# A four-layer graph network on one core: node steps one to a group and tied behind the group's messages, carried sums on TensorE, ranks by a predicated copy

## The chip, the cores and the metric

The kernel runs on one core of one Trainium2 chip. The metric is the device time of one execution in microseconds. The profiled execution of the kernel before took 5402.67 us and its span, from the first to the last instruction that the profiler saw, is 5400.9 us. Engine names are those of the profile: PE is TensorE (PEld its weight loads), DVE is VectorE, ACT is ScalarE, POOL is GpSimd, SP is SyncE, which here only issues transfers.

## The reference

The node features `x` are 6250 x 160 (64 scalars and 32 three-vectors a node). There are 100000 edges, each with a source `src` and a target `dst`, and the edges come sorted by `dst`. Four layers follow each other, each of the form `x = x + gnn(relu(layernorm(x)))`. Cut to what the change touches, a layer is

```
gs, gv   = lin1(h)[src]                         # gather a row of a table for each edge
weight   = silu(edge_features @ W_fc1) @ W_fc2  # 192 weights for each edge
edge_msg = [w0*gs*ys, w3*dot(gv, yv), w1*gs*yv, w2*gv*ys]        # 384 numbers an edge
agg      = segment_sum(edge_msg, dst, N)
x        = x + lin2(agg) + skip(h)
```

The third layer (index 2) gathers by `dst` and sums by `src` instead, so that its edges have to be put in the order of `src` first: each edge needs its rank in that order.

## The kernel before

The edges stand in 784 tiles of 128, and 14 tiles make a **window**. All edges of a window point to at most 128 nodes that follow each other, and column 0 of a window is the node that the window before may have begun. There are 56 windows. A **group** is 4 tiles, so that a layer has 196 groups and a window is 3.5 groups long.

Layers 0, 1 and 3 run in `edges(li)`. Its main loop takes one group after the other and records, in this order:

- `prepare` (L1363): the loads of a pair of windows (`load`, SP queue), and the gather of the group that is 6 ahead: 4 indirect transfers of 128 rows on POOL (L1280);
- `weights_of` and `edge_weights`: on PE the hidden layer `ph` (L1269; L1263 in layer 3) and the weights `pw` (L1303; L1296 in layer 3), on ACT the activation (L1272) and the copies to `ws` (L1307, L1309);
- `messages`: seven DVE instructions, the one-hot `oh` (L1322), `pr` (L1333), `dot` (L1334) and four parts of `msg` (L1336, L1339, L1340 and, as the last one recorded, L1341);
- the sum over edges: 4 products `pg` (L1397) with the one-hot as weights. After the last tile of a window ACT copies the sums to `acc` (L1400), and a Python generator `nodes` (L1346) for this window joins the list `live`;
- the node work: each generator in `live` is advanced. Every `yield` in it ends a step.

The steps of a window's node work are, in `nodes` and `nodes_out`: the one-hot `turn` (L1349, DVE) and four products `pt_out` (L1062, PE) that turn and shift `acc`; the copy `at` (L1069, ACT) and the addition of the sums that the window before has left for this window's first node (L1073, DVE: column 0 of the `at` before into column 1 of this one); the products `po` (L1080, L1082, PE); and the update of `xt` (L1095, L1096, DVE; in layer 3 a chain from L1115 on with a sine on ACT, L1135). Layers 0 and 1 go on in `nodes_in` with the next layer's input: statistics (L991, L992, DVE), `norm` with small instructions of 0.15 us to 0.27 us (L886, L969 to L979, L888, DVE), `hn` (L999, ACT), in layer 0 `hk` (L1004, DVE), the transposes `pt_in` (L1009, L1010, PE), their copies `ht` (L1013, L1014, ACT), the products `pa` (L1022, PE), the table's rows `tb` (L1031 or L1033, ACT), and in layer 0 the addition of `pa` to `xt` (L1041, DVE), with the writes to memory on the SP queue (L1034, L1047, L1048). All `pt_out`, `po`, `pt_in` and `pa` tiles share two PSUM buffers.

Beside layers 0 and 1 runs `positions` (L1142), the ranks by `src`. For each of 54 buckets it makes a mask `hit` over all 784 tiles (L1166), a running count `cum` (L1168), and takes the count over where the mask is set by a product and a sum (L1171, L1172). After every third group of layers 0 and 1 one step of it is recorded.

The engines do not run in the order of recording. A scheduler (the tile framework) puts the instructions of each engine in an order when the program is built: of what is ready by its own estimate, what was recorded first goes first. On the chip each engine then works through its fixed order, and an instruction that waits holds up all that is queued behind it. Between layers stands a full dependence: a layer's gathers read the table that the node work before has written, to the last window.

Two stages between layer 1 and layer 3, `messages2` and `sums2`, do the third layer; `sums2` uses `nodes_out` without `turn`.

Of the kernel before, what the change touches and what calls it, by code (L numbers as in the profile page):

```python
# [11 lines left out]
F32 = mybir.dt.float32  # L12
# [3 lines left out]
ALU = mybir.AluOpType  # L16
# [673 lines left out]
class Fast:  # L690
# [360 lines left out]
    def nodes_out(self, li, xt, sk, acc, turn, carry, w, wk, pp):  # L1051
# [5 lines left out]
        for k in range(4):  # L1057
            rows, o = (96, 3 * MV) if k == 0 else (MV, (k - 1) * MV)
            if turn is None:
                nc.tensor.transpose(pt[:rows, k, :], acc[:, o : o + rows], self.ident[:n, :n])  # L1060
            else:
                nc.tensor.matmul(pt[:rows, k, :], lhsT=acc[:, o : o + rows], rhs=turn, start=True, stop=True)  # L1062
        yield
# [4 lines left out]
        else:  # L1068
            nc.scalar.copy(at, pt)  # L1069
        if turn is not None:  # L1070

            if carry[0] is not None:
                nc.vector.tensor_add(at[:, :, 1], at[:, :, 1], carry[0][:, :, 0])  # L1073
            carry[0] = at
        yield
# [66 lines left out]
    def positions(self, wk):  # L1142
# [21 lines left out]
        for b in range(BK + 1):  # L1164
            hit = wk.tile([P, TT], BF16, name="hit2", bufs=2)
            nc.vector.tensor_scalar(hit, self.src_b, float(b), None, op0=ALU.is_equal)  # L1166
            cum = wk.tile([P, TT], F32, name="cum", bufs=2)
            nc.vector.tensor_tensor_scan(cum, hit, self.zero.to_broadcast([P, TT]), self.off[:, b : b + 1], op0=ALU.add,  # L1168
                                         op1=ALU.add)
            yield  # L1170
            nc.vector.tensor_mul(cum, cum, hit)  # L1171
            nc.vector.tensor_add(pos, pos, cum)  # L1172
            yield
# [31 lines left out]
    def edges(self, li):  # L1205
# [31 lines left out]
        def load(u):  # L1237

            rt = ld.tile([P, 2 * WT, 8], F32, name="rt")
            nc.sync.dma_start(rt.rearrange("p t c -> p (t c)"), self.a["rec0"][u])  # L1240
            rows = self.a[f"ft{li}"].shape[1]
            ft = ld.tile([rows, self.a[f"ft{li}"].shape[2]], F32, name="ft")
            nc.sync.dma_start(ft, self.a[f"ft{li}"][u])
            for h in range(2):
                k = 2 * u + h
                at = self.at(k)
                xt = nk.tile([P, XW], F32, name="xt", bufs=10)
                nc.sync.dma_start(xt, self.x[li][ds(at, P), :])
                sk = None
                if li == 3:  # L1250
                    sk = nk.tile([P, 160], F32, name="sk_out", bufs=10)
                    nc.sync.dma_start(sk, self.skip[3][ds(at, P), :])
                xts[k] = xt, sk
            data[u] = rt, ft
# [57 lines left out]
        def messages(u, g):  # L1312
# [27 lines left out]
            tt(mvec[:, :, :, 0:64], by3(t1, 64), yv[:, :, :, None].to_broadcast([P, n, 3, 64]), ALU.mult)  # L1340
            tt(mvec[:, :, :, 64:96], e1, by3(ws[:, :, 64:96], 32), ALU.mult)  # L1341
            return oh, msg

        carry = [None]

        def nodes(k, acc):  # L1346
            xt, sk = xts.pop(k)
            turn = nk.tile([P, P], F32, name="turn")
            nc.vector.tensor_scalar(turn, self.iota, self.column[:, k : k + 1], None, op0=ALU.is_equal)  # L1349
# [35 lines left out]
        for i, (u, g) in enumerate(groups):  # L1385
            prepare(i + AHEAD)
            weights_of(i + 2)
            if i + 1 < len(groups):
                edge_weights(*groups[i + 1])
            oh, msg = messages(u, g)  # L1390
            for k in range(width(u, g)):
# [6 lines left out]
                if end:  # L1398
                    acc = wk.tile([P, AW], F32, name="acc")
                    nc.scalar.copy(acc, pg)  # L1400
                    live.append(nodes(t // WT, acc))
            data.pop(u - 1, None)
            live = [n for n in live if not (next(n, True) or next(n, True))]
            if li < 2 and i % 3 == 0:
# [363 lines left out]
```

## Time and profile before

| what | us |
|---|---|
| three runs | 5421.51, 5421.99, 5408.77; median 5421.51 |
| profiled execution, and its span | 5402.67, 5400.9 |
| before the loop of layer 0 | 0 to 160 |
| layer 0 with its node work | 160 to 1320 |
| layer 1 with its node work | 1320 to 2440 |
| `messages2`, `sums2` | 2440 to 3525, 3525 to 4340 |
| layer 3 | 4340 to 5401 |
| busy over the span | PE 4493.4, DVE 4198.7, ACT 2075.5, POOL 3192.6 |

The start of the last message product of a group (L1341) gives the pace: in layer 0 the first is at 181.6 and the 196th at 1304.7, in layer 1 at 1337.6 and 2414.6, in layer 3 at 4364.5 and 5379.5. Divided by the 195 steps between them that is 5.76, 5.52 and 5.21 us a group.

How to read the views: a group of instructions is one row with its line, engine, operation, tiles and shapes, how many there were, their busy time and the mean of one in ns, and then the idle time of that engine just before them with what ended it. A row of the waits says which instruction waited for which, in total, how often, and the longest. A row of the stages gives a stretch with the busy time (and number) of PE, PEld, DVE, ACT and POOL, then the clock granted to PE as a share of its full one, the DMA share and GB/s. The ends of PE's instructions are modelled, so that PE's busy time says more than its work.

### The profile page before, as it was taken

How to read it: one execution, taken by the hardware profiler on the slowest of the kernel's cores; microseconds unless marked ns; L12 is line 12 of the kernel's file. 1: busy time of each engine (PE TensorE's matmuls, PEld its weight loads, DVE VectorE, ACT ScalarE, POOL GpSimd, SP SyncE). 2: the span in 40 equal slices, each digit the busy share in tenths (PEclk: the TensorE clock that was granted, in tenths of full speed). 3: DMA queues.
4: the chain of work that ended last, by engine and by line, in shares of the span. 5: the costliest groups of instructions: out<-in, count | busy, mean ns of one | idle time of the engine just before them, and what ended most of it. 6: DMA issues, size and time to landing. Idle time of an engine off the chain costs nothing.

```text
span 5400.9 us, 77388 instructions
## 1 busy us (share of the span) xinstructions
PE 4493.4 (83%) x22084; PEld 2812.5 (52%) x22084; DVE 4198.7 (78%) x11742; ACT 2075.5 (38%) x6858; POOL 3192.6 (59%) x3143
## 2 busy tenths in 40 slices
PE   6899999998999999985565565589999988888886
PEld 4455555554455555543443344368888844444443
DVE  6688888987888888975777777767777768878787
ACT  5444444443444444543333333312222244444442
POOL 0577777773777767765777777700000057777776
PEclk9988998988888888986777776689999978888887
DMA  3333333322333333326655656477777533333332
GB/s 96 111 94 92 89 87 89 88 75 69 95 94 89 96 85 91 99 75 201 205 199 201 211 194 207 161 276 238 239 235 237 186 81 84 82 85 85 84 80 58
DMA packets 373006, 708.23 MB, mean 131 GB/s; under 512 B 71469, under 2 KB 250890, under 8 KB 372442
## 3 DMA queue, kind: packets, MB, share of 16 engines
q0 software_dynamic: 163072, 349.43, 22.4%
q1 hardware_dynamic: 208914, 353.42, 21.3%
q8 instruction: 180, 2.95, 0.2%
q14 instruction: 256, 2.10, 0.1%
q10 hardware_dynamic: 584, 0.33, 0.0%
HBM read 493.90 MB, written 209.08 MB: 130 GB/s over the span
## 4 chain that ended last, share of the span: by engine, by line
PE 23%; DVE 11%; DMA 11%; POOL 8%; issue 5%; ACT 2%; SPq 0%; DVEq 0%; ACTq 0%; POOLq 0%
PE pg L1620 7%; DMA rec<-row,edge_to 6%; PE pg L1618 5%; DMA ge<-table,rt 5%; POOL rec L1516 5%; POOL ge L1280 3%; PE pg L1397 2%; DVE msg L1340 2%; PE pa L1022 1%; PE po L1082 1%; DVE msg L1336 1%; DVE row L1509 1%; DVE pr L1333 1%; PE ph L1458 1%; PE pw L1296 1%
## 5 line engine op out<-in xcount | busy, mean ns | idle before, releaser
L1280 POOL DMA_INDIRECT ge<-table,rt x2352 | 2374.6, 1010 | 1878.2 <-DMA skip<-sk 830.3
L1397 PE MATMUL pg<-msg,oh 128*64 128x384 f32 x4704 | 1072.5, 577 | 159.6 <-DVE msg L1341 144.1
L1307 ACT ACTIVATE ws<-pw,rt 128x96 f32<-128x96 f32 x2352 | 691.8, 349 | 843.3 <-DVE msg L1341 320.1
L1516 POOL DMA_INDIRECT rec<-row,edge_to x784 | 817.2, 1042 | 302.3 <-issue 182.1
L1303 PE MATMUL pw<-w_w2y,hh 100*128 100x192 f32 x3136 | 676.7, 358 | 16.5 <-ACT ws L1309 14.1
L1397 PEld LDWEIGHTS pg<-msg,oh 128*64 128x64 f32 x4704 | 310.9, 151 | 721.3 <-issue 262.4
L1303 PEld LDWEIGHTS pw<-w_w2y,hh 100*128 100x128 f32 x3136 | 545.1, 205 | 224.6 <-ACT ws L1309 110.2
L1340 DVE TENSOR_TENSOR msg<-msg,bank 128x768 f32<-128x768 f32 x588 | 556.2, 946 | 0.0
L1620 PE MATMUL pg<-msg,oh 128*120 128x288 f32 x1668 | 541.3, 406 | 0.0
L1336 DVE TENSOR_TENSOR msg<-ws,ge 128x512 f32<-128x512 f32 x588 | 402.7, 685 | 71.6 <-DMA ge<-table,rt 71.3
L1484 PE MATMUL pe<-tb,oh 64*128 64x160 f32 x1568 | 280.3, 416 | 200.8 <-ACT row L1493 198.7
L1618 PE MATMUL pg<-rt,oh 128*120 128x192 f32 x1668 | 410.1, 328 | 35.1 <-DVE oh L1608 35.1
L1272 ACT ACTIVATE hh<-ph 100x1024 f32<-100x1024 f32 (+1 forms) x336 | 269.5, 802 | 406.4 <-PE pw L1296 179.7
L1333 DVE TENSOR_TENSOR pr<-ge,bank 128x384 f32<-128x384 f32 x588 | 320.4, 545 | 125.2 <-DMA ge<-table,rt 124.2
L1484 PEld LDWEIGHTS pe<-tb,oh 64*128 64x128 f32 x1568 | 211.4, 259 | 354.9 <-ACT row L1493 344.7
L1269 PE MATMUL ph<-ft,w_w1r 12*100 12x512 f32 (+1 forms) x784 | 328.9, 666 | 78.5 <-ACT hh L1272 60.2
L1309 ACT COPY ws<-pw 128x192 f32<-128x192 f32 x1176 | 390.4, 332 | 0.0
L1458 PE MATMUL ph<-ft,w_w1d 128*128 128x512 f32 x224 | 176.8, 887 | 239.4 <-ACT hh L1460 215.9
L1618 PEld LDWEIGHTS pg<-rt,oh 128*120 128x120 f32 x1668 | 298.1, 184 | 123.2 <-issue 36.3
L1509 DVE TENSOR_TENSOR row<-pw,ev 128x512 f32<-128x512 f32 x196 | 135.4, 691 | 282.8 <-ACT row L1495 270.2
L1334 DVE TENSOR_REDUCE dot<-pr 128x128 f32<-128x384 f32 x588 | 344.4, 586 | 0.1
L1341 DVE TENSOR_TENSOR msg<-ge,ws 128x384 f32<-128x384 f32 x588 | 324.4, 552 | 0.0
(488 smaller groups left out, 7439.9 us busy)
## 6 DMA issues: line engine op xcount, KB each, us to landing
rt<-rec SPq DMA_DIRECT2D x208, 780.0 KB
ge<-table,rt POOLq DMA_INDIRECT x2352
ft<-in_ft_dram SPq DMA_DIRECT2D x56, 512.0 KB
ft<-in_ft_dram SPq DMA_DIRECT2D x28, 896.0 KB
dt<-in_dst_w_dram SPq DMA_DIRECT2D x112, 224.0 KB
xt<-x SPq DMA_DIRECT2D x168, 82.0 KB
rec<-row,edge_to POOLq DMA_INDIRECT x784
rt<-in_rec_dram SPq DMA_DIRECT2D x84, 112.0 KB
```

The costliest lines, as they stand in the source:

```text
L1280: nc.gpsimd.indirect_dma_start(out=ge[:, k, :], out_offset=None, in_=self.table[li], in_offset=bass.IndirectOffsetOnAxis(ap=rt[:, G * g + ...
L1303: nc.tensor.matmul(pw[:, i, :192], lhsT=hh[:, k + i, :], rhs=w2, start=True, stop=True)
L1307: nc.scalar.activation(ws[:, k0 + i, 0:96], pw[:, i, 0:96], AF.Copy, scale=rt[:, G * g + k0 + i, 0:1])
L1309: nc.scalar.copy(ws[:, k0 : k0 + m, 96:192], pw[:, :m, 96:192])
L1333: tt(pr, e1, yv[:, :, :, None].to_broadcast([P, n, 3, 32]), ALU.mult)
L1336: tt(msg[:, :, AW - 64 : AW + 64].rearrange("p g (k u) -> p g k u", k=2), ws.rearrange("p g (k u) -> p g k u", k=2)[:, :, :, 0:64], e0[:, ...
L1340: tt(mvec[:, :, :, 0:64], by3(t1, 64), yv[:, :, :, None].to_broadcast([P, n, 3, 64]), ALU.mult)
L1397: nc.tensor.matmul(pg[half], lhsT=oh[:, k, :], rhs=msg[:, k, :AW], start=t % WT < 2, stop=t % WT >= WT - 2)
L1484: nc.tensor.matmul(pe[:, 2 * h + k // 2, :160], lhsT=oh[rows, (t0 + k) % WT // 2, :], rhs=tb[rows], start=True, stop=True)
L1516: d = nc.gpsimd.indirect_dma_start(out=self.rec2, out_offset=bass.IndirectOffsetOnAxis(ap=self.edge_to[:, t0 + k : t0 + k + 1], axis=0), i ...
L1618: nc.tensor.matmul(pg[:, 0:192], lhsT=oh[:, k, :], rhs=rt[:, k, 0:192], start=first, stop=end, skip_group_check=True)
L1620: nc.tensor.matmul(pg[:, 192:480], lhsT=oh[:, k, :], rhs=msg[:, k, :], start=False, stop=end, skip_group_check=True)
```

## The change

Three things, all in the part of the program that layers 0, 1 and 3 share.

First, the list `live` is advanced once a group, not twice, and inside a context that puts an ordering edge from the group's last message product to every DVE instruction that the steps record: the scheduler cannot put them in front of it. Instructions of other engines get no edge. Since a window's node work now lasts twice as many groups, its tiles get more buffers (`xt` and `sk_out` 14 for 10, `turn` and `acc` 6 for 2).

Second, the carried sums are no longer added by DVE behind the copy `at`. The generator keeps the window's `acc` and `turn`, and in the next window PE adds, for each of the four parts of `pt_out`, a product of the old `acc` with column 0 of the old `turn` into column 1 of the same PSUM tile.

Third, in `positions` the product and the sum become one predicated copy: where `hit` is not zero, `pos` takes `cum`.

```
             rows, o = (96, 3 * MV) if k == 0 else (MV, (k - 1) * MV)
             if turn is None:
                 nc.tensor.transpose(pt[:rows, k, :], acc[:, o : o + rows], self.ident[:n, :n])
-            else:
-                nc.tensor.matmul(pt[:rows, k, :], lhsT=acc[:, o : o + rows], rhs=turn, start=True, stop=True)
+                continue
+            nc.tensor.matmul(pt[:rows, k, :], lhsT=acc[:, o : o + rows], rhs=turn, start=True, stop=carry[0] is None,
+                             skip_group_check=True)
+            if carry[0] is not None:
+                sums, turned = carry[0]
+                nc.tensor.matmul(pt[:rows, k, 1:2], lhsT=sums[:, o : o + rows], rhs=turned[:, 0:1], start=False,
+                                 stop=True, skip_group_check=True)
+        if turn is not None:
+            carry[0] = acc, turn
         yield
...
             nc.scalar.copy(at, pt)
-        if turn is not None:
-            if carry[0] is not None:
-                nc.vector.tensor_add(at[:, :, 1], at[:, :, 1], carry[0][:, :, 0])
-            carry[0] = at
         yield
...
-            nc.vector.tensor_mul(cum, cum, hit)
-            nc.vector.tensor_add(pos, pos, cum)
+            nc.vector.copy_predicated(pos, hit.bitcast(mybir.dt.uint16), cum)
...
-                xt = nk.tile([P, XW], F32, name="xt", bufs=10)
+                xt = nk.tile([P, XW], F32, name="xt", bufs=14)
...
-                    sk = nk.tile([P, 160], F32, name="sk_out", bufs=10)
+                    sk = nk.tile([P, 160], F32, name="sk_out", bufs=14)
...
-            tt(mvec[:, :, :, 64:96], e1, by3(ws[:, :, 64:96], 32), ALU.mult)
-            return oh, msg
+            last = tt(mvec[:, :, :, 64:96], e1, by3(ws[:, :, 64:96], 32), ALU.mult)
+            return oh, msg, last
...
-            turn = nk.tile([P, P], F32, name="turn")
+            turn = nk.tile([P, P], F32, name="turn", bufs=6)
...
-                    acc = wk.tile([P, AW], F32, name="acc")
+                    acc = wk.tile([P, AW], F32, name="acc", bufs=6)
                     nc.scalar.copy(acc, pg)
                     live.append(nodes(t // WT, acc))
             data.pop(u - 1, None)
-            live = [n for n in live if not (next(n, True) or next(n, True))]
+            with tc.issue_after(last.ins):
+                live = [n for n in live if not next(n, True)]
             if li < 2 and i % 3 == 0:
                 next(self.sort, None)
```

More of the change, by code (lines that the diff above doesn't have):

```diff
@@ L1389, in edges @@
                 edge_weights(*groups[i + 1])
-            oh, msg = messages(u, g)
+            oh, msg, last = messages(u, g)
             for k in range(width(u, g)):
```

## The prediction

> **What bounds the kernel now.** I read the stages first, then two short stretches against each other, then DVE's waits, then POOL. The stages show where the change can act: 160 to 1320 is layer 0, then layer 1, and the last row is layer 3. `messages2` and `sums2` (1900 us together) keep their instructions and are left out.
>
> ```profile
> 160.00:1320.00 1160.00, 1062.94 (x5119) 612.57 (x5120) 996.55 (x2779) 525.17 (x1642) 803.43 (x784) 0.91 0.34 89
> 1320.00:2440.00 1120.00, 1024.79 (x4770) 577.37 (x4769) 928.88 (x2642) 510.44 (x1728) 792.58 (x784) 0.88 0.35 92
> ...
> 4340.00:5401.00 1061.00, 876.38 (x4280) 455.20 (x4280) 821.16 (x2458) 414.65 (x1472) 778.64 (x784) 0.85 0.32 81
> ```
>
> PE (first busy time) looks like the bound of layers 0 and 1, at 92%, but its granted clock is only 0.91 and 0.88. The next view says how much of that is work. Both rows are layer 1; in the first the ranks (`positions`) are finished, whose last instructions are at 2125 us, in the second they run.
>
> ```profile
> 2180.00:2320.00 140.00, 137.32 (x746) 80.78 (x743) 129.84 (x396) 79.95 (x270) 107.71 (x107) 0.99 0.37 97
> 1900.00:2040.00 140.00, 129.40 (x567) 72.02 (x568) 114.00 (x321) 60.98 (x207) 92.32 (x94) 0.84 0.33 85
> ```
>
> Without the ranks, 30 groups (instances of L1341) pass in 140 us, 4.67 us each; with them 23, 6.1 us. PE has the same work a group in both. So PE at its full clock needs at most 4.67 us a group in layer 1, and what stretches it to 5.8 is DVE: its work, and its waits, during which PE idles and cools. The waits of DVE, layer 0 and then layer 1:
>
> ```profile
> DVE xt L1041 <- ACT tb L1033: 47.3, 18, 6.4
> DVE at L1073 <- ACT at L1069: 44.0, 30, 6.7
> DVE xt L1095 <- PE po L1082: 29.9, 41, 7.2
> DVE hk L1004 <- ACT hn L999: 19.3, 16, 5.7
> DVE pr L1333 <- DMA ge<-table,rt: 11.4, 3, 8.5
> ```
>
> ```profile
> DVE at L1073 <- ACT at L1069: 119.7, 42, 10.8
> DVE xt L1095 <- PE po L1082: 24.3, 34, 1.2
> ```
>
> They are the node steps: DVE stands at the addition of the carried sums until PE has turned `acc` and ACT has copied it. One such wait in the order of time, near the end of layer 0:
>
> ```profile
> 1292.86 1.88 PEld L1062 LDWEIGHTS pt_out<-turn,acc 128*96 128x96 f32 x8
> ...
> 1295.13 0.58 ACT L1069 COPY at<-pt_out 96x512 f32<-96x512 f32 x1 [1.41 <-PE pt_out L1062]
> ...
> 1295.75 0.16 DVE L1073 TENSOR_TENSOR at<-at 96x4 f32<-96x4 f32 x1 [6.67 <-ACT at L1069]
> 1295.83 0.55 DVE L1341 TENSOR_TENSOR msg<-ge,ws 128x384 f32<-128x384 f32 x1
> ```
>
> An addition of 0.16 us holds DVE for 6.67 us with a message product (L1341) queued behind it, and PE's next `pg` waits for that product.
>
> POOL is the floor. In layer 3 DVE waits for gathers (L1333 101.9 us, L1336 67.3 us), and POOL does nothing but issue them:
>
> ```profile
> L1280 POOL DMA_INDIRECT ge<-table,rt x784 | 778.6, 993 | 1068.8 <-DMA skip<-sk 830.3 <-issue 176.7 <-DMA ge<-table,rt 14.0
> ```
>
> 993 ns and 0.30 us of issue, four to a group, are 5.17 us, and layer 3 runs at 5.21. In layer 0 one takes 1009 ns (580 to 720 us), so 5.24 us a group. The stretch at 4.67 was fed by gathers up to 6 groups ahead: POOL did 107 in it, 26.8 groups' worth, while DVE used 30.
>
> **The change, part by part.**
>
> *Waits.* In the queues of the changed program I counted, in groups from a window's last `pg`, where its node instructions stand. Before, `po` stands on PE at 0.75 and the update of `xt` on DVE at 1.0, with the addition in between; after, `po` at 0.3 and the update at 3.0, and no addition. The addition of `pa` to `xt` (L1041) comes at 5.0 before, with `pa` at 3.6, and at 10.0 after, with `pa` at 7.15. So the waits 44.0, 29.9 and 47.3 of layer 0 and 119.7 and 24.3 of layer 1 go; `hk` stays three DVE instructions behind `norm`, and its 19.3 I keep. The added edge makes node instructions wait behind L1341; queued behind them are only the next group's messages, as before, and the ones that need node results (`hn` and `hk`, PE's `pt_in`) have groups in hand. `po` and `pa` hold their PSUM buffers for 2.7 groups instead of 0.25 to 1.4. `pt_in`, at 6.5, follows the releases of both on DVE, also at 6.5 (3.0 and 10.0 less a window of 3.5): free, with nothing to spare. The SP queue's loads run three pairs of windows ahead, and the extra `xt` buffers keep that.
>
> *DVE's work.* 165 additions of 0.161 us go, 9 us a layer. Of the ranks, 54 pairs of 0.966 and 0.967 us go, 31 of them in layer 0 and 23 in layer 1. The predicated copy is not in the trace. Over the same 784 numbers the cheapest row is the mask (L1166, 363 ns) and the dearest the scan (L1168, 1840 ns): a saving of 1.57 us at most and 0.09 at least, 85 us or 5 in all. I take 0.967, the row of two streams read and one written, which is what it does: 30 us saved in layer 0, 22 in layer 1. DVE's layer 0 is then 996.6 - 30 - 9 + 19 + 11 = 988 us with the waits that stay (the 11 for gathers), 5.04 us a group; layer 1 is 929 - 22 - 9 + 15 = 913, 4.66.
>
> *PE's work.* 660 one-column products come in, four a window, each with its own weights of 96 columns, in two passes. At least nothing (in PE's idle time), at most as dear as the `pt_out` beside them in the fence above, 1.9 us a window at the slow clock. The nearest row is the smallest product of the same weight shape (L947, 96 x 96 weights on 32 columns): four passes in 0.48 us. So eight passes 0.96 us a window, 0.27 us a group. `ph` is cut in two more often by the new order (209 single rows in PE's queue for 145): 32 pairs no longer run beside each other, at 1.10 us each 35 us over 392 groups, 0.09 us. Layer 0 has `pa` and `pt_in` for two copies of `h`: 1.63 + 0.60 us a window (at 1311.0 and 655.0) against layer 1's 1.13 + 0.39 (at 1807.4 and 2310.9), so 0.20 us a group above 4.67. PE then needs 4.67 + 0.20 + 0.27 + 0.09 = 5.23 us in layer 0, and 5.03 in layer 1, at its full clock.
>
> [...]
>
> *Sum.* What is late next in layer 0 is PE (5.23) and POOL (5.24) together, in layer 1 POOL (5.24) with PE behind it. Three engines so close do not all run without gaps, so I take 3% and 2% more: 5.42 and 5.33 us. Layer 0: (5.76 - 5.42) x 195 = 66 us less. Layer 1: (5.52 - 5.33) x 195 = 37 us less. Layer 3: POOL's 5.21 stays; DVE's 46.6 us of node waits there lie beside its waits for gathers. Each loop's end gets longer: the window before the last has its statistics, `norm` and `hk` still ahead instead of half done (about 4 us by the end of layer 0, where the rest of `norm` to `hk` took 1305.2 to 1309.2), in front of the last window's own chain; 4 + 4 + 2 = 10 us. In all -66 - 37 + 10 = -93 us: 5310 us against the profiled 5402.67. Scaled to the median (5421.51), 5328 us.
>
> **Rivals.**
>
> *The floor is reached.* Layers 0 and 1 both at 5.24, ends 6 us longer: -101 - 55 + 6 = -150, 5253 against the profile, 5271 by the median. For it: layer 3 holds POOL's pace. Against: PE at 96% and more.
>
> *Waits only change places.* DVE's waits stay as long in total, for `hn`, PSUM or gathers, and only its work counts: -39 - 31 + 10 = -60, 5361. With a predicated copy as dear as the scan it is -18 - 5 + 10 = -13, 5408: no change.
>
> *Slower: PE stays cold and is the bound.* `pg` takes 1.51 us for a group at the full clock and 2.83 us at 1305.34, after PE stood 2.20 us. If PE keeps a mean clock of 0.91 and 0.88, its 5.23 and 5.03 become 5.75 and 5.72 us: nothing won in layer 0, (5.72 - 5.52) x 195 = 39 us lost in layer 1, 10 at the ends, and 0.27 / 0.85 = 0.32 us a group more in layer 3, where a fifth would show (12 us): 61 us, 5483 by the median. It decides from a mean clock of 0.91 in layer 0. For it: PE is busy 92% already. Against: the stretch at 0.99, where DVE had shorter waits.
>
> [...]
>
> **The numbers.** Forecast 0.42, floor 0.15, waits change places 0.16, no change 0.10, slower 0.17. What this measurement can tell from no change is about 0.3%, 16 us: faster 0.73, same 0.10, slower 0.17. The range goes from below the floor's case with a cheap predicated copy (5255) to past the case of no change (5430); it leaves out the slower case.
>
> **What would show it.** Right: the waits at L1041 and L1095 nearly gone, PE's clock in layers 0 and 1 above 0.93, POOL's idle time almost all issue, 5.3 to 5.45 us a group, layer 3 unmoved. Wrong: new DVE waits for `hn` or PSUM of 50 us or more a layer; one-column products above 1.5 us a window; a predicated copy near 1.8 us.

## The result, and the profile after

The changed kernel takes 5462.44 us (median of 4 runs, 5454.7 to 5472.35) where the kernel before took 5417.33 on the same chip (4 runs): ratio 1.0086, 95% interval 1.0063 to 1.0109. **It is slower by 0.9%**; the forecast was 5328, with a range up to 5430. Its profiled execution has a span of 5464.2 us, 63.3 more than the one before.

Where the 63.3 us are, by the ends of the last message product of a group (L1341 before, L1343 after) of the first and the 196th group of each loop:

| stretch | before | after | difference |
|---|---|---|---|
| to the first group of layer 0 | 182.2 | 182.6 | +0.4 |
| layer 0, 195 groups | 1123.1 | 1151.3 | +28.2 |
| from layer 0's last to layer 1's first | 32.8 | 46.0 | +13.2 |
| layer 1, 195 groups | 1077.0 | 1082.9 | +5.9 |
| from layer 1's last to layer 3's first | 1949.9 | 1963.1 | +13.2 |
| layer 3, 195 groups | 1015.1 | 1016.3 | +1.2 |
| from layer 3's last to the end | 20.8 | 22.0 | +1.2 |

Three lines answer to the stages before, and the fourth to the short stretch of layer 1 without the ranks (columns as there):

```profile
160.00:1340.00 1180.00, 1112.88 (x5508) 669.94 (x5508) 952.75 (x2654) 518.11 (x1620) 794.18 (x784) 0.90 0.31 87
1340.00:2500.00 1160.00, 1077.97 (x5261) 635.30 (x5260) 906.99 (x2604) 522.32 (x1750) 787.16 (x784) 0.88 0.32 89
4400.00:5464.00 1064.00, 939.83 (x4720) 516.57 (x4720) 819.10 (x2409) 408.64 (x1472) 779.85 (x784) 0.81 0.30 81
2260.00:2400.00 140.00, 137.24 (x746) 80.61 (x744) 118.21 (x357) 73.04 (x249) 107.34 (x108) 1.00 0.31 84
```

DVE's busy time in layer 0 fell from 996.6 to 952.8 us, as forecast. The granted clock did not rise: 0.90 and 0.88 where it was 0.91 and 0.88. The short stretch is the only one at 1.00, and there 28 groups pass in 140 us, 5.0 us each, where it was 4.67: PE is busy 137 of 140 us in both, so its work for a group has grown.

DVE's waits for node steps, layer 0 and then layer 1:

```profile
DVE hk L1004 <- ACT hn L999: 204.7, 52, 11.3
DVE pr L1335 <- DMA ge<-table,rt: 12.9, 3, 9.1
```

```profile
DVE xt L1098 <- PE po L1085: 175.1, 33, 13.8
DVE pr L1335 <- DMA ge<-table,rt: 33.5, 17, 11.1
DVE xt L1041 <- ACT tb L1033: 11.0, 2, 7.1
DVE hk L1004 <- ACT hn L999: 3.8, 1, 3.8
```

The addition at L1073 no longer exists and the wait at L1041 is down from 47.3 to 11.0 us. (The last node steps of layer 0 run after 1340, so the waits at L1041 and the 3.8 us at `hk` in the second list are layer 0's.) But `hk` went from 19.3 to 204.7 us, and the update of `xt` in layer 1 from 24.3 to 175.1. One such wait in the order of time, in layer 1:

```profile
1790.86 1.33 PE L1271 MATMUL ph<-ft,w_w1r 10*100 10x512 f32 x2 [1.17 <-ACT hh L1274]
...
1791.55 0.55 DVE L1343 TENSOR_TENSOR msg<-ge,ws 128x384 f32<-128x384 f32 x1
...
1792.12 1.55 PE L1399 MATMUL pg<-msg,oh 128*64 128x384 f32 x4
1792.15 0.28 DVE L1351 TENSOR_SCALAR turn<-iota,column 128x128 f32<-128x128 f32 x1
...
1796.66 0.74 PE L1062 MATMUL pt_out<-turn,acc 128*96 128x128 f32 x2
1796.99 0.50 PEld L1067 LDWEIGHTS pt_out<-turn,acc 128*96 128x96 f32 x2
1797.20 0.37 PE L1067 MATMUL pt_out<-turn,acc 128*96 128x1 f32 x2
...
1799.85 0.58 ACT L1077 COPY at<-pt_out 96x512 f32<-96x512 f32 x1 [5.17 <-PE pt_out L1067]
...
1805.32 0.91 PE L1085 MATMUL po<-w_v,at 96*128 96x96 f32 x6
...
1806.27 0.28 DVE L1098 SCALAR_TENSOR_TENSOR xt<-po,am,xt 128x64 f32<-128x64 f32 x1 [13.84 <-PE po L1085]
```

The first line is PE's wait of 1.17 us for the buffer of `ph`, which ACT's `hh` empties. DVE does its last message product, `turn`, and then stands 13.84 us at the update of `xt` (L1098), the longest of its kind. It is easily read as "PE and ACT are late with this chain". The same stretch, cut in four, says what PE did:

```profile
1789.00:1792.00 3.00, 1.83 (x7) 0.64 (x5) 3.00 (x6) 1.94 (x5) 2.39 (x3) 0.93 0.36 107
1792.00:1799.00 7.00, 7.00 (x26) 4.07 (x25) 0.43 (x3) 0.93 (x3) 5.17 (x7) 0.50 0.45 134
1799.00:1806.00 7.00, 7.00 (x27) 4.45 (x27) 0.00 (x0) 1.84 (x7) 5.38 (x6) 0.55 0.30 78
1806.00:1810.00 4.00, 3.78 (x22) 2.25 (x21) 3.73 (x11) 2.31 (x9) 3.18 (x3) 1.00 0.30 83
```

PE was busy for 14.00 of the 14 us in which DVE waited, at a clock of 0.50 and 0.55, and back at 1.00 when DVE went on. DVE waits because PE works at half its clock through everything in front of `po`, also through the `pg` of two groups whose messages DVE had finished (`msg` has four buffers, so DVE runs up to three groups ahead: in 22 of the 392 groups of layers 0 and 1 the `pg` of three earlier groups was unfinished when DVE ended a group's last message product, in 116 that of two). So I split each loop, in steps of 1 us, into **work** (PE's busy time times the granted clock: what it would need at full clock), **cold** (busy time times what is missing from the clock), and **idle** (the rest; the ends of PE's records are modelled, so all three are estimates, each from the one profiled execution of a kernel). The number and summed length, inside the loop, of the stretches in which the clock stood at half stand behind it, by the trace's clock records, which know only 1.00 and 0.50. DVE's busy time is in the last column.

| kernel, loop | length | work | cold | idle | cold stretches | DVE busy |
|---|---|---|---|---|---|---|
| before, layer 0 | 1123 | 939 | 105 | 79 | 34, 215 us | 979 |
| after, layer 0 | 1151 | 985 | 116 | 51 | 24, 232 us | 942 |
| before, layer 1 | 1077 | 876 | 119 | 82 | 42, 248 us | 917 |
| after, layer 1 | 1083 | 919 | 110 | 54 | 25, 220 us | 887 |
| before, layer 3 | 1015 | 726 | 129 | 160 | 46, 274 us | 810 |
| after, layer 3 | 1016 | 748 | 172 | 96 | 34, 366 us | 805 |

In layers 0 and 1 PE was idle for 79 and 82 us in all. That was all that shorter waits of DVE could give back directly, and 28 us of it came in each. Against it stand 46 and 43 us of new work on PE, at a clock that stayed where it was. The stretches at half clock are fewer but longer: 9.7 and 8.8 us in the mean instead of 6.3 and 5.9. In layer 3 the same happens beside POOL's gathers, and costs nothing.

The lines of the parts themselves, in the groups of the changed kernel (busy us, mean ns; idle time and what ended it):

```profile
L1067 PEld LDWEIGHTS pt_out<-turn,acc 128*96 128x96 f32 x1320 | 217.9, 194 | 0.0
...
L1067 PE MATMUL pt_out<-turn,acc 128*96 128x1 f32 x1320 | 186.2, 210 | 0.0
...
L1077 ACT COPY at<-pt_out 96x512 f32<-96x512 f32 x168 | 97.8, 582 | 410.7 <-PE pt_out L1067 407.5 <-PE pt_out L1062 3.2
...
L1174 DVE COPY_PREDICATED pos<-hit,cum 128x784 f32<-128x784 uint16 x54 | 55.3, 1025 | 0.0
```

A predicated copy takes 1.025 us, close to the 0.967 taken. A one-column product holds PE for 210 ns, and its weights load in 194 ns beside the one in front (both means over full and half clock; where the clock was full the loads took 163 ns). ACT now waits 407.5 us for `pt_out`; at L1069 it was 190.3 before.

### The profile page after: what moved, and what is told of

Its sections match the earlier page's. It is cut to its first block, busy times and chain, and to the rows that moved or that the text cites. A ratio compares the mean times of both kernels' runs of the same rounds, so it can differ in the third digit from the quotient of the medians.

```text
span 5464.2 us, 79891 instructions
## 1 busy us (share of the span) xinstructions
PE 4673.3 (86%) x23404; PEld 2996.2 (55%) x23404; DVE 4130.0 (76%) x11523; ACT 2075.0 (38%) x6858; POOL 3180.7 (58%) x3143
## 4 chain that ended last, share of the span: by engine, by line
PE 20%; DMA 11%; DVE 9%; POOL 8%; issue 5%; ACT 2%; SPq 1%; DVEq 0%; ACTq 0%; POOLq 0%
PE pg L1623 7%; DMA rec<-row,edge_to 6%; PE pg L1621 5%; DMA ge<-table,rt 4%; POOL rec L1519 4%; POOL ge L1282 3%; PE pg L1399 1%; PE pa L1022 1%; DVE row L1512 1%; DVE msg L1338 1%; PE pw L1298 1%; DVE msg L1342 1%; PE ph L1461 1%; PE po L1085 1%; DVE dot L1336 1%
## 5 line engine op out<-in xcount | busy, mean ns | idle before, releaser
L1305 PE MATMUL pw<-w_w2y,hh 100*128 100x192 f32 x3136 | 693.6, 357 | 25.5 <-ACT ws L1311 22.9
L1271 PE MATMUL ph<-ft,w_w1r 12*100 12x512 f32 (+1 forms) x784 | 359.4, 654 | 82.8 <-ACT hh L1274 67.6
L1062 PE MATMUL pt_out<-turn,acc 128*96 128x128 f32 x1344 | 322.4, 342 | 1.3 <-ACT acc L1402 1.2
```

What stands on the lines that cost most here:

```text
L1305: nc.tensor.matmul(pw[:, i, :192], lhsT=hh[:, k + i, :], rhs=w2, start=True, stop=True)
```

## The experiments

The theories, by the letters that the expectations use. **A**: PE is the bound of layers 0 and 1; its work counts, and its cold clock multiplies it. **B**: DVE is the bound, and its waits for node steps only changed place. **C**: the order of one step a group costs, whatever PE does. D, E and F came with later runs. All ratios are to the kernel before, run beside them on the same chip, with their 95% interval.

**The three parts alone, and the changed kernel without its products.** First the predicated copy alone, in the kernel before:

```
-            nc.vector.tensor_mul(cum, cum, hit)
-            nc.vector.tensor_add(pos, pos, cum)
+            nc.vector.copy_predicated(pos, hit.bitcast(mybir.dt.uint16), cum)
```

> The kernel before with the predicated copy alone (54 pairs of about 0.97 us become 54 copies of 1.03, about 49 us of VectorE work less, all in layers 0 and 1). Theory A, TensorE is the bound of layers 0 and 1 (its work at full clock 939 and 876 us, idle only 79 and 82 us, the rest a cold clock): VectorE's work is off the path, so 0 to 20 us are gained, ratio 0.996 to 1.000. Theory B, VectorE is the bound and its waits for node steps only changed place: most of the 49 us are gained, ratio 0.991 to 0.993. Theory C (the order of one step a group costs) says nothing of this run.

Measured: 5334.62 us, ratio 0.9856 (0.9832 to 0.988), 74 us faster by the medians: more than either theory said, and more than the 49 us that DVE saves. Both loops, 183 to 1267 and 1309 to 2351 us, columns as in the stages:

```profile
183.00:1267.00 1084.00, 1015.57 (x5038) 588.93 (x5036) 951.23 (x2671) 512.22 (x1610) 795.86 (x776) 0.93 0.35 90
1309.00:2351.00 1042.00, 972.34 (x4663) 549.64 (x4661) 898.70 (x2579) 496.84 (x1688) 788.73 (x777) 0.91 0.37 95
```

PE's work stayed (940 and 888 us). Cold went from 105 to 75 and from 119 to 84, idle from 79 to 68 and from 82 to 70. So DVE's work does count, and by this split most of what it gave back was cold clock and not idle time.

Then the carried sums on PE alone (the diff's second part, with `acc` and `turn` in 6 buffers), and the single step with its tie alone (its first part, the addition left on DVE):

> The kernel before with the carried sums on TensorE alone (660 one-column products, the addition on VectorE gone, acc and turn in 6 buffers so that they live long enough); two steps a group and no tie, as before. Theory A: about 0.7 us of TensorE work a window come in, 38 us a layer, in layers 0 and 1 where it is the bound; VectorE's waits at the addition go and return little: 40 to 80 us slower, ratio 1.007 to 1.015, and work at full clock in layers 0 and 1 up by 30 to 40 us each. Theory B: the waits at the addition (44 and 120 us) go, and others come: 0 to 60 us faster, 0.989 to 1.000. Theory C: the products are neutral, 0.997 to 1.003.

> The kernel before with one node step a group, tied behind the last message, and its larger pools, alone; the addition of the carried sums stays on VectorE. Theory A: TensorE's work hardly changes (only the splits of ph, 5 to 15 us a layer) while the ends grow by 20 to 26 us: between 10 us faster and 40 slower, ratio 0.998 to 1.007. Theory B: VectorE's waits for node steps in layers 0 and 1 sum to what they were (285 us) or more: ratio 1.000 to 1.006. Theory C: this part carries the whole loss, 1.007 to 1.012.

Measured: the carry 5564.63 us, ratio 1.0264 (1.0238 to 1.029); the step 5485.02 us, 1.0137 (1.0115 to 1.016). The carry costs twice what A expected: work is up by 28 and 58 us in layers 0 and 1, and cold by 26 and 46. That falsifies B and C for this part. The step costs too, in layer 0 (53 us more: work 15, cold 34) and at the ends (16 and 10 us); in layer 1 it took 3 us less, with 26 us more work and 27 us less cold. C's own run came out just above what C said (1.007 to 1.012), but not as the whole loss: the three parts multiply to 1.026, and the whole is 1.0086, so they are not independent.

> The changed kernel without the one-column products and without the additions they replaced: the carried sums between windows are left out of the computation, so that only the price of the products shows. Theory A: 38 us of TensorE work go from each of layers 0 and 1, some 20 from layer 3, which has slack: 60 to 100 us faster than the changed kernel, ratio to before 0.990 to 0.998. Theory B: the chain from acc to the updated xt gets shorter by the 0.7 to 1.2 us that the products lengthen pt_out, 1 us in each of 110 windows at most and partly hidden: 10 to 50 us faster than the changed kernel, 0.999 to 1.007. Theory C: hardly moved, 1.006 to 1.010.

```
-            carry[0] = acc, turn
+            carry[0] = None
```

Measured: 5334.27 us, ratio 0.9859 (0.9843 to 0.9875), 128 us below the changed kernel by the medians (the kernel before took 5408.91 and 5417.33 beside them), more than all had expected. Against the changed kernel, layers 0 and 1 lose 64 and 61 us: 30 and 37 us of work, 36 and 46 of cold, and idle time rises by 2 and 22. The 55 windows of a layer make 0.55 and 0.67 us of work a window: as work, the products are **cheaper than the 0.96 us forecast**; what they cost in time is nearly twice their work, since the clock is lower with them. The cold stretches are 6.7 and 5.0 us long without them (24 and 27, 162 and 134 us), and 9.7 and 8.8 with them. (The expectation of the next run has 225 us in 23 and 147 us in 23 for layer 0: it left out a stretch that runs past the loop's end.)

**Why the clock is lower with them.** A product of one column streams that one column behind a weight load of 194 ns (the rows of L1067 above). Theory **D** supposes that such time does not bring the clock back up, so that a stretch at half clock goes on through it; what the array does inside a product stands in no trace, so D can only be tested by time and clock. The test is to make the products dearer.

```
-                nc.tensor.matmul(pt[:rows, k, 1:2], lhsT=sums[:, o : o + rows], rhs=turned[:, 0:1], start=False,
+                nc.tensor.matmul(pt[:rows, k, :], lhsT=sums[:, o : o + rows], rhs=turned, start=False,
```

> The changed kernel with each carried product 128 columns wide instead of one: the right side is the whole of turned and all of pt_out takes the sum, so every sum of a window gets the former window's added (the computation is changed). It asks why the clock's cold stretches are longer with the products (225 us in 23 stretches of layer 0, 9.8 us each, against 147 in 23, 6.4 each, in the run without them). Theory D, a product of one column leaves the array idle behind its weight load and doesn't count as activity, so the clock stays low: with 128 columns the stretches fall to 5 to 7 us, 30 us less cold time a layer, for 10 to 22 us more work (four products beside four of pt_out, 0.9 to 1.1 us instead of 0.7): ratio to before 1.000 to 1.007. Theory A, work added in a cold stretch simply takes twice as long and the stretch lasts by the stalls: 20 to 45 us a layer more, 1.013 to 1.025.

Measured: 5318.68 us, ratio 0.9815 (0.9801 to 0.983), far below D's 1.000 to 1.007: 2.7% below the changed kernel, with 128 columns where that has one. Work is up by 14 and 35 us, and cold is down from 116 and 110 to 32 and 38. Theory A without D is out.

Its order on PE differs too. Theory **F** is that the order made it. Three runs were made against F. Two put useless products on another base, the kernel before with the predicated copy, with no carry and no change of steps; their sources differ only in the width of the products:

```
-                nc.tensor.matmul(pt[:rows, k, :], lhsT=acc[:, o : o + rows], rhs=turn, start=True, stop=True)
+                nc.tensor.matmul(pt[:rows, k, :], lhsT=acc[:, o : o + rows], rhs=turn, start=True, stop=False,
+                                 skip_group_check=True)
+                nc.tensor.matmul(pt[:rows, k, :128], lhsT=acc[:, o : o + rows], rhs=self.zeros[:, :128], start=False,
+                                 stop=True, skip_group_check=True)
```

> The kernel before with the predicated copy (ratio 0.9856 without more), and behind each of pt_out's four products a useless one of one column: the same weights on one column of zeros, added to pt_out, so that the result stays and nothing but the product is new (no carry, no change of steps, VectorE's addition kept). Theory D, products of one column keep the clock low: like the carried products, 60 to 130 us slower than without, ratio 0.997 to 1.012, and cold stretches of 8 to 10 us. Theory A, the work alone counts, at up to twice its 38 us a layer: 40 to 130 us, 0.993 to 1.010; stretches of 6 to 8 us.

> The same, but the useless products have 128 columns of zeros: more work by the durations (273 ns each for 217). Theory D, what counts is how long the array streams: the clock rises sooner, and the useless work is won back in part or whole, between 20 us faster and 30 slower than the predicated copy alone, 0.982 to 0.991, and below the one with one column. Theory A: the most work, so the slowest of the three: 1.000 to 1.015. Theory F, what made the wide carried products fast was the other order of TensorE's queue (or the sums it changed), not their width: no clear difference to the one with one column, within 0.004 of it.

Measured: with one column 5466.32 us, 1.0102 (1.0079 to 1.0124); with 128 columns 5333.5 us, 0.9852 (0.983 to 0.9874), the same as with no useless products at all (0.9856). The wide ones came out as D said; A (1.000 to 1.015) and F (within 0.004 of the narrow ones) did not. The run with one column lies in D's range and at the edge of A's. Layers 0 and 1 of the first and of the second:

```profile
183.00:1325.00 1142.00, 1080.25 (x5476) 650.32 (x5476) 956.02 (x2672) 512.21 (x1610) 801.82 (x775) 0.91 0.34 86
1358.00:2460.00 1102.00, 1037.64 (x5098) 614.59 (x5100) 897.89 (x2579) 499.27 (x1687) 783.59 (x776) 0.89 0.35 89
```

```profile
183.00:1282.00 1099.00, 1070.73 (x5480) 634.85 (x5480) 955.53 (x2673) 509.21 (x1610) 797.55 (x775) 0.95 0.35 89
1319.00:2355.00 1036.00, 1001.77 (x5103) 581.72 (x5104) 898.28 (x2582) 500.75 (x1688) 789.00 (x777) 0.95 0.37 95
```

The number of PE's instructions agrees within five (5476 and 5480; 5098 and 5103), and DVE's work is the same. The order of PE's instructions is not the same, though F's forecast took it to be, so that these two runs do not rule F out by themselves. The wide ones are the longer ones, by their rows in the two runs:

```profile
L1064 PE MATMUL pt_out<-zeros,acc 128*96 128x1 f32 x1344 | 187.3, 209 | 0.0
```

```profile
L1064 PE MATMUL pt_out<-zeros,acc 128*96 128x128 f32 x1344 | 271.8, 286 | 0.0
```

The clock, third from the end of the loops' lines, is 0.91 and 0.89 with one column, 0.95 and 0.95 with 128. Work rises by 39 and 33 us with the width; cold falls by 48 and 68, idle by 34 and 30.

The third run, and a fourth, keep the reference's result on the changed kernel: ScalarE writes a right side that is zero but for its second column (`self.second` is one there and zero elsewhere), and the product takes it whole (its output is then `pt[:rows, k, :128]`; in the third run 32 stands for 128). `turn`, which no longer has to outlive its window, goes back to the pool's two buffers.

```
+            wide = wk.tile([n, 128], F32, name="wide", bufs=3)
+            nc.scalar.activation(wide, self.second[:, :128], AF.Copy, scale=turn[:, 0:1])
-            carry[0] = acc, turn
+            carry[0] = acc, wide
```

> The changed kernel with its carried products 32 columns wide: ScalarE writes a right side that is zero but for the second column, which is turned's first, so that the result stays the reference's; 55 copies more on ScalarE a layer. Theory D: by the columns streamed, between one column (1.0086) and 128 (0.9815), and nearer to one column: 0.998 to 1.008. Theory F: anywhere between 0.98 and 1.02, out of line with the widths.

> The same with 128 columns: the changed kernel whose carried products are wide and whose result is the reference's. Theory D: as the wide products before, which changed the sums: 0.979 to 0.986, layer 0's cold stretches under 100 us in all. Theory F: anywhere between 0.98 and 1.02; theory A: 1.010 to 1.025.

Measured: 32 columns 5359.72 us, 0.9904 (0.9885 to 0.9922); 128 columns 5333.7 us, 0.986 (0.9833 to 0.9887). For 1, 32 and 128 columns the ratio is 1.0086, 0.9904 and 0.986, and layer 0's and 1's cold time 116 and 110, 66 and 63, 39 and 38 us. Layers 0 and 1 with 128:

```profile
183.00:1253.00 1070.00, 1048.03 (x5452) 628.07 (x5452) 943.05 (x2605) 530.86 (x1662) 785.00 (x775) 0.96 0.36 91
1297.00:2316.00 1019.00, 992.00 (x5086) 578.46 (x5082) 889.67 (x2514) 513.14 (x1739) 777.01 (x776) 0.96 0.37 96
```

On two bases, in five runs of three widths, time and cold clock follow the width, which leaves F little room; 32 columns do more of it than D expected. **The wide products cost as much time as none** (0.9859 without them), though they are 72 us more work in layer 1 (954 for 882). In layer 1 that has a second reason: both runs stand at POOL's pace there, 5.23 and 5.24 us a group, with POOL idle for little else than the 0.30 us of issue in front of each gather (779.1 us of gathers and 236.4 idle without the products; with 128 columns as below):

```profile
L1286 POOL DMA_INDIRECT ge<-table,rt x776 | 777.0, 1001 | 236.5 <-issue 197.5 <-DMA ge<-table,rt 7.6 <-DVE pr L1339 6.4
```

**What the clock follows.** No run was made for this; it is read from 14 traces, the kernel before, the changed one and the twelve runs described so far and in the next two sections. In their clock records every one of the 732 stretches at half clock that begin in the loops of layers 0 and 1 lasts a whole multiple of 3.413 us. For each window of that length, in step with the records and wholly inside these loops, I added up, over PE's instructions, rows times columns of the weights times streamed columns. By its shape an instruction of `pg` adds 3.15 million, one of `pt_out` 1.57, one of `ph` 0.61 or 0.51, and a carried product of one column 0.01. The clock of the next window goes by this sum:

| sum in a window, millions | at full clock: half clock follows | at half clock: half clock follows |
|---|---|---|
| under 20 | 466 of 468 | 351 of 365 |
| 20 to 23 | 197 of 217 | 244 of 259 |
| 23 to 25.5 | 62 of 194 | 125 of 310 |
| 25.5 to 28 | 0 of 324 | 11 of 326 |
| over 28 | 0 of 6197 | 0 of 210 |

A line at 24 million gets 8675 of the 8870 windows right, in kernels whose orders on PE differ, so F is not needed. PE's busy share does not tell the windows at half clock apart: 97% in the mean where half clock follows, 98% where full clock does. In the stretch above, the window from 1788.19 us, with the wait of 1.17 us and a `ph`, has 21.8; the four at half clock from 1791.60 have 21.7, 20.8, 15.8 and 29.3, and then the clock is full. So D holds in a sharper form: a product of one column keeps PE busy for 210 ns and adds 1/128 of what one of 128 columns adds. That the sum itself is what the chip counts stays a reading of the traces; a quantity that goes with it would look the same.

**What starts a cold stretch.** Of the 34 that begin in layer 0 before, 27 have a wait of `ph` for `hh` in the six us in front, and 28 of 42 in layer 1; after, 18 of 24 and 19 of 25. Such six us are 16% to 28% of the loops, so this is far above chance. The first timeline above shows one: PE idles 1.17 us, and at 1791.60, 0.74 us after that, the clock halves. The seven groups of a pair of windows make three pairs and one single `ph`, which stands one group from its neighbour. So I took pairs across that end:

```
-                if g % 2 == 0:
-                    hidden(u, g // 2)
+                if i % 2 == 0:
+                    hidden(i)
```

> The kernel before with the predicated copy, and with the hidden rows (ph) taken in pairs of groups that run across the end of a pair of windows, so that no group of the seven stands alone: 98 pairs instead of 84 pairs and 28 single ones a layer. Its base is the run with the predicated copy alone, ratio 0.9856. Theory A with the cold clock's cause named: 27 of 34 cold stretches of layer 0, and 28 of 42 of layer 1, begin right behind a wait of ph for hh of about 1 us, 28 times a layer, where the single ph follows or leads a pair one group apart; without it 27 us of waits, 15 to 30 us of TensorE work and 30 to 50 us of cold clock go from each of layers 0 and 1: 0.955 to 0.975. Theory E, the cold stretches come anyway, by the next stall of pg or pw: only the work goes, 0.975 to 0.983. Theory B: TensorE is not the bound, 0.984 to 0.988.

Measured: 5356.15 us, ratio 0.9892 (0.9875 to 0.9908): a miss for A and E, and at best the upper end of B's range. The waits of `ph` did not go: 28 waits with 29.2 us in layer 0 and 33 with 37.7 in layer 1, where its base, the predicated copy alone, has 23 with 19.8 and 37 with 29.7. Work and cold stayed (951 and 77, 888 and 97 us). So it tells nothing of Theory **E**, that other stalls would take their place; that the waits start the stretches is not shown by a run. By the sums above the wait is only part of it: in the last full-clock window before a stretch, before and after the change, PE stands for 0.8 to 1.2 us in the mean, and is busy with `ph`, which adds next to nothing, for another 1.0 to 1.6.

**The step and the tie.** Two more of the combinations of the diff's parts, copy and step and then copy and carry:

> The changed kernel with the addition of the carried sums put back on VectorE, and the products gone: one step a group with its tie, and the predicated copy. If parts add, 0.9856 x 1.0137 = 0.999. Theory A (TensorE's work and its cold clock decide, and VectorE's waits only matter where they stall TensorE): near the run without any carried sums, 5334 us, and 9 us of additions a layer and their waits on top: 0.986 to 0.995. Theory B (waits of VectorE for node steps, wherever they stand, are the loss): VectorE stands at the addition again, one instruction group sooner than it can be done: 0.998 to 1.006.

> The kernel before with the predicated copy and the carried sums on TensorE; two steps a group and no tie. What the changed kernel has beyond this is the step and the tie. If parts add, 0.9856 x 1.0264 = 1.012, and the step's order is then worth 0.003 less than nothing. Theory A: 1.005 to 1.012, with work at full clock in layers 0 and 1 of 965 and 920 to 935 us. Theory C (one step a group costs, as it did alone, 1.0137): 0.990 to 0.998.

Measured: predicated copy and step 5385.85 us, 0.9947 (0.9932 to 0.9962); predicated copy and carry 5496.37 us, 1.0142 (1.0126 to 1.0158). The first is at the upper end of A's range and below B's; the second is a little above A's and far from C's. With the earlier runs each part has a price on several bases (a ratio over the ratio of its base; each good to some 0.3%):

| part | alone | with copy | with carry | with step | with both others |
|---|---|---|---|---|---|
| predicated copy | -1.4% | | -1.2% | -1.9% | not run |
| carry on PE, one column | +2.6% | +2.9% | | not run | +1.4% |
| one step and tie | +1.4% | +0.9% | not run | | -0.6% |

The copy gains everywhere and the carry costs everywhere. The sign of the step depends on the carry: it costs while DVE still stands at the addition, and gains 0.6% when PE holds the products (layer 1 then takes 1083 us for 1155, the latter in the slowest of that kernel's five executions). Which of its two halves does that, fewer steps or the tie, was to be told by the first two of three last runs; the third asks whether streaming elsewhere wins more of the clock. It is the kernel before with the predicated copy (0.9856) and, ahead of each pair's hidden rows in layers 0 and 1, four useless bf16 products of 128 weights on 256 columns of zeros, written to unused columns of `bank`. No trace here gives the time of such a product, so the 100 us of work that Theory A names for it are a supposition of mine.

```
-            with tc.issue_after(last.ins):
-                live = [n for n in live if not next(n, True)]
+            live = [n for n in live if not next(n, True)]
...
             else:
+                for _ in range(4):
+                    nc.tensor.matmul(bank[:, 256:512], lhsT=self.zeros[:, :P], rhs=self.zeros, start=True, stop=True)
                 ph = p_h.tile([H, 2, 4, P], F32, name="ph")
```

> The changed kernel without the tie: one node step a group, free to be scheduled ahead of the group's messages. If the tie is what costs in the order, 0.995 to 1.004; if it only fixes what the scheduler would do anyway, within 0.004 of the changed kernel's 1.0086.

> The kernel before with the predicated copy and with carried products of 128 columns (zero but for one), two steps a group and no tie; with one column it took 1.0142. Theory D: 0.980 to 0.990, as the width did for the changed kernel, cold stretches under 130 us a layer. Theory F (the order decides, not the width): 1.005 to 1.02. Held against the changed kernel with the same wide products, 0.986: if it is faster by over 0.003, one step a group with its tie costs time by itself; if slower, it gains.

> [...] Theory D: the clock stays up, the cold 75 and 84 us fall to under 45 each, and some of the work lies in waits: 0.975 to 0.990. Theory A: work is added where TensorE is the bound, 100 us or more: 1.003 to 1.03.

They were run twice (s_notie, s_pcwide and s_fillph the second time, with the same expectations), and are inconclusive: the kernel before itself took 6898 and 7058 us beside them. ScalarE stood there for long times at a releaser that the profile can't name ("remote" in the rows), for instance in the last of the three:

```profile
ACT acc L1403 <- remote: 377.3, 60, 11.2
ACT ws L1310 <- remote: 336.8, 43, 27.9
...
ACT hh L1275 <- remote: 291.9, 43, 26.6
```

None of these waits is in the other runs. The ratios there were 1.0406 and 1.0338 without the tie, 1.0018 and 1.0005 with wide products and two steps, 0.9875 and 0.9869 with useless products before `ph`. With ScalarE held up like this and no run of the changed kernel beside them they decide nothing about the kernels at 5410 us. What the tie does alone, and whether more of the cold clock can be won, stays open.

**What beats both kernels by most, with the reference's result**: the predicated copy alone (0.9856), and the changed kernel with carried products 128 columns wide (0.986), which agree within their intervals. The first is the smaller change.

## Why the prediction was wrong

- **What bounds the kernel: wrong, and this is the step that failed.** "What stretches it to 5.8 is DVE: its work, and its waits, during which PE idles and cools." PE was idle for 79 of 1123 us in layer 0 and 82 of 1077 in layer 1. The 0.94 and 1.03 us a group above PE's work (184 and 201 us over 195 groups) were mostly a cold clock (105 and 119 us), and it doesn't need DVE's long waits: in the traces it comes after a window with too little work in it and stays while the work is light (half clock followed in 1258 of the 1309 windows with a sum under 23 million), however busy PE is. So new work of the lightest kind, the one-column products, met a clock that stayed at 0.90 and 0.88, and cost more than the shorter waits gave back.
- **"So the waits ... go": wrong.** They changed place, 204.7 us at `hk` (forecast to stay at 19.3) and 175.1 at the update of `xt` (forecast to go). I took the distance in the queues, 3.0 groups, for time. DVE runs up to three groups ahead of PE, so those 3.0 groups are about none, and `hk`, three instructions behind `norm`, had nothing at all. The timeline shows the rest for the longest of them: DVE waits while PE works at half clock.
- **DVE's work: right.** 37 and 30 us less in the two loops, forecast 39 and 31; the predicated copy 1.025 us, taken 0.967. That it alone would bring 74 us was not seen.
- **PE's work: nearly right.** 0.55 and 0.67 us a window for the products at full clock, taken 0.96. The rows of their loads have 163 ns each at the full clock, eight a window, and lie partly beside other products. `ph` got 30.5 us more busy time by more splits (359.4 for 328.9), taken 35. PE's work a group is 5.05 and 4.71 us (985 and 919 over 195), below the 5.23 and 5.03: their base, 4.67 from a stretch with some idle time, was an upper bound (the split gives 4.49 in layer 1 before), and the additions were smaller (0.22 for 0.36 there).
- **The sum: wrong.** "3% and 2% more" stood for everything that PE loses besides its work. It is 167 and 164 us after the change, 15% of the loop. (3% and 2% on 5.24 are also 5.40 and 5.34, not 5.42 and 5.33; that is 2 us in all.)
- **POOL as the floor: right, though the change did not reach it.** Layer 1 runs at 5.24 us a group without the products and at 5.23 with wide ones, as forecast for the floor.
- **The ends: right in sign, too small.** 13.2 + 13.2 + 1.2 = 27.6 us, taken 10.
- **Layer 3: right**, +1.2 us: POOL's gathers cover 22 us more work and 43 more cold on PE there.
- **The slower rival, "PE stays cold and is the bound", came about**, by its own condition: a clock of 0.90 and 0.88, and 5.0 us a group in the only stretch at full clock. Its total of 61 us agrees with the measured 63 by luck: it has 0 + 39 us for the two loops, where 28 + 6 were measured, 10 at the ends for 28, and 12 in layer 3 for 1. What spoke for it, PE busy 92% of the time, outweighed what I set against it, one stretch of 140 us.
- **The `pg` of 2.83 us behind 2.20 us of idle time: misread.** The prediction has the slow `pg` at 1305.34 us come after the idle time in front of it. By the clock records the clock had halved at 1302.00 us, before those 2.20 us began at 1303.14, and behind an idle time of 2.59 us. Nor does it take idle times of that length: after the change PE never stands for more than 1.61 us in the loops of layers 0 and 1, and its clock halves 48 times there. A busy window was not enough to end a cold stretch either: the 24 that lie wholly in layer 1's loop after the change are 3.41, 6.83, 10.24, 13.65 or 17.07 us long, one to five times 3.413, and from 1791.60 to 1805.25 PE was busy throughout while the clock stayed at half for four windows. The sums above say what was missing.

## What to carry to other kernels

Before a wait is priced, split the bound engine's time into work at full clock, cold clock and idle: only the idle part is what a shorter wait gives back directly, and a wait on another engine may be no more than the sight of TensorE at half speed (above, 14.00 of 14 us of such a wait, at a clock of 0.50 and 0.55). Products of one column are not cheap on a TensorE whose clock goes back and forth between full and half, since in these traces the clock went by the size of the products in a window and not by PE's busy time: here 128 columns behind the same weights took 2.2% off the time against one, so when a small product can be widened for nothing, or an engine with slack can do it, measure that first. A distance between two instructions in the queues is free time only after the lead that one engine has on the other is taken off it.

## What the runs showed of the hardware that was not expected

- Useless products of one column cost 132 us (5466.32 for 5334.62 by the medians, with the kernel before at 5413.56 and 5408.91 beside them; 1.0102 for 0.9856 as ratios), and useless products of 128 columns nothing (0.9852).
- The clock of a window of 3.413 us went by the sum of rows times columns times streamed columns in the window before: under 23 million half clock followed in 1258 of 1309 windows, over 25.5 million in 11 of 7057, with PE busy 97% to 98% of the time at half clock either way.
- 49 us less work on VectorE took 74 us off a kernel whose TensorE was busy 92% of the time in those layers, with the same work there: the cold time fell by 65 us.
- The predicated copy of 784 four-byte numbers a partition with a two-byte mask takes 1.025 us, 6% more than a product of the same size (0.966).
- In two sets of runs the kernel before took 27% and 30% longer than in the others, with hundreds of us of waits of ScalarE for something that the trace doesn't name.
